# Turned blocks of three norms: through DRAM instead of sixteen moves a group

## The chip, the cores and the metric

The kernel runs on one core of one Trainium2 chip. The metric is the device time in microseconds, the median of three runs. The core has five engines that work side by side, each through its own list of instructions in order: TensorE (PE) multiplies matrices, VectorE (DVE) and ScalarE (ACT) work element by element, GpSimd (POOL) does smaller element work, and SyncE (SP) issues DMA transfers. POOL issues some transfers too. An instruction that has to wait for another engine or a transfer holds whatever stands behind it on its own engine.

## The reference

Four layers are applied to an x of 2 x 1024 tokens by 512 features, each as x + layer(layernorm(x)), in single precision:

```
x = x + attn_a(layernorm(x))     # gated linear attention in chunks of 128, 4 heads
x = x + ffn(layernorm(x))        # 512 -> 1408 -> 512, weights as codes and scales
x = x + attn_b(layernorm(x))     # softmax attention, one head of width 512
x = x + ffn(layernorm(x))        # the same weights again
ffn(x): down(silu(gate(x)) * up(x))
layernorm(x): (x - mean) / sqrt(var + 1e-5), without weights
```

The norms are called a, f, b and g after the layers that they feed.

## The kernel before, in words

Tokens are worked on in 16 tiles of 128. Four tiles make a group (index `st`, 0 to 3), two groups a pair (`pr`, 0 and 1). All products take operands with features on the partitions, so every normed tile has to be turned. Each large product splits its single-precision operand into a rounded high part and the rest (`split`, lines 75 and 76: a copy on ACT, then a subtraction on DVE that reads that copy).

The f, b and g norms are made by `ln_steps`, eight steps for each group. Four `ln_norm` steps, one for each tile, load the tile (line 102), norm it (lines 109 to 122; two tiny instructions run on POOL) and turn it on DVE in blocks of 32 x 32 (line 198). DVE turns each block where it stands, so the result `y` still has its blocks in the wrong partitions. `y` has one buffer, `[128, 4, KD, ST, 32]`: for a partition, 4 target blocks `b`, 4 feature tiles `k`, 4 tiles `i` of the group, 32 tokens `q`. Then four `ln_move` steps (`b` = 0 to 3) put the blocks in place with four transfers each, from SBUF to SBUF (line 209). Each takes 32 partitions to 32 partitions, 64 KB in runs of 32 elements. The result `xT` sits in one of 12 slots of 1 MB (`slot`), which are shared with weights and operands. SP issues the moves of a and f, of groups 0 and 1 of b, half of group 2 of b, and group 3 of g; POOL issues the others.

`combine` then forms, for a pair of groups, the operands of a scheme with seven products in place of eight. B11 and B12 are the lower half of the features of the pair's first and second group, B21 and B22 the upper halves. Its steps split B11, B21, B22 (for b also B12) and the sums T1, T2, T3, T4 into operand slots (`T_f`, `B_f` and so on in the profile); `less` (line 257) makes the sums in place in `xT` on DVE. `products` (line 338) and `score_product` (line 1023) multiply with them.

Where these steps stand in the order is written out by hand. In attention A a table (`fill`) gives each step of norm f a chunk. In the two FFNs a `plan` says how many steps follow each of the 11 blocks of hidden columns, and each of the eight output tiles. In attention B `do(norm, n)` and `do(moving, n)` place them between products. `behind(...)` puts the instructions of a step after given ones on the same engine. Within that, a planner orders every engine's instructions by a costing of its own.

The neighbours on the queues are: in attention A the row loads and the x1 stores; in the FFNs the weight loads `wcf`/`wcg` (line 327), residual loads `xrf`/`xrg` and output stores; in attention B the probabilities. Those are turned on DVE in blocks too (line 1100), stored to DRAM (`p<-py`, line 1104) and loaded back in four parts (`ptl<-p`, line 1116).

Of the kernel before, what the change touches and what calls it, by code (L numbers as in the profile page):

```python
# [9 lines left out]
F32 = mybir.dt.float32  # L10
# [6 lines left out]
P = 128  # L17
# [8 lines left out]
ST = 4  # L26
# [8 lines left out]
def hybrid_block_kernel(ctx: ExitStack, tc: tile.TileContext, a, out):  # L35
    nc = tc.nc
# [7 lines left out]
    dp = ctx.enter_context(tc.tile_pool(name="dram", bufs=1, space=bass.MemoryType.DRAM))  # L44
# [5 lines left out]
    def slot(name, dt=F32R):  # L50

        return wp.tile([P, 2048], dt, tag="slot", name=name)
# [20 lines left out]
    def split(hi, lo, src, eng=None):  # L73

        c = nc.scalar.copy(hi, src)  # L75
        return c.ins, (eng or nc.vector).tensor_tensor(lo, src, hi.bitcast(F32), ALU.subtract).ins  # L76
# [106 lines left out]
            low.dma_start(out=dst[m][:, 512:1024], in_=lo.bitcast(F32))  # L183
        return done

    lnT, lnY, lnX, laid = {}, {}, {}, []

    def ln_norm(src, nm, st, i):

# [10 lines left out]

    def ln_move(nm, st, b):

        if b == 0:
            lnT[nm, st] = slot(f"xT_{nm}{st}").rearrange("p (k c) -> p k c", k=KD)
        y = lnY[nm, st]
        xf = lnT[nm, st].bitcast(F32).rearrange("p k (i b q) -> p (k i) b q", i=ST, b=4)
        for c in range(4):
            sync = nm in "af" or (nm, st) in (("b", 0), ("b", 1), ("g", 3)) or ((nm, st) == ("b", 2) and c % 2)
            (nc.sync if sync else nc.gpsimd).dma_start(  # L209
                out=xf[32 * b : 32 * (b + 1), :, c, :],  # L210
                in_=y[32 * c : 32 * (c + 1), b].rearrange("p k i q -> p (k i) q"),
            )
# [12 lines left out]
    def ln_steps(src, nm, st):  # L225

        return [lambda i=i: ln_norm(src, nm, st, i) for i in range(ST)] + [
            lambda b=b: ln_move(nm, st, b) for b in range(4)
        ]
# [12 lines left out]
    def combine(nm, pr):  # L242


        B = {}

        def begin():
            ra, rb = (lnT[nm, 2 * pr + n].bitcast(F32) for n in range(2))
            B.update(B11=ra[:, 0:2], B12=rb[:, 0:2], B21=ra[:, 2:4], B22=rb[:, 2:4])

        def part(n, src):
            o = slot(f"{n}_{nm}{pr}").rearrange("p (s k c) -> p s k c", s=2, k=2)
            XT[nm, pr, n] = o
            split(o[:, 0], o[:, 1], B[src])

        def less(dst, x, y):
            nc.vector.tensor_tensor(B[dst], B[x], B[y], ALU.subtract)

        if nm == "b":

            return [
                lambda: (begin(), part("B11", "B11")),
                lambda: part("B21", "B21"),
                lambda: part("B12", "B12"),
                lambda: part("B22", "B22"),
                lambda: less("B11", "B12", "B11"),
                lambda: part("T1", "B11"),
                lambda: less("B12", "B22", "B12"),
                lambda: part("T3", "B12"),
                lambda: less("B22", "B22", "B11"),  # L270
                lambda: part("T2", "B22"),
                lambda: less("B21", "B21", "B22"),
                lambda: part("T4", "B21"),
            ]
        return [
            begin,
            lambda: part("B11", "B11"),
            lambda: less("B11", "B12", "B11"),
            lambda: part("T1", "B11"),
            lambda: part("B22", "B22"),  # L280
            lambda: less("B12", "B22", "B12"),
            lambda: less("B22", "B22", "B11"),
            lambda: part("T2", "B22"),
            lambda: part("T3", "B12"),
            lambda: part("B21", "B21"),
            lambda: less("B21", "B21", "B22"),
            lambda: part("T4", "B21"),
        ]
# [59 lines left out]
    with ExitStack() as actx:  # L348
# [11 lines left out]
            out=le, in_=ones, compare_op=ALU.is_ge, fill=0.0, base=0, pattern=[[1, P]], channel_multiplier=-1  # L360
# [592 lines left out]
    with ExitStack() as bctx:  # L953
# [247 lines left out]
        for b in range(NB):  # L1201
            nm, src, g = ("b", x2, 2) if b == 0 else ("g", x3, 0)
# [138 lines left out]
```

## Time and profile before

| | us |
|---|---|
| median of three runs (least, most) | 927.1 (926.89, 927.81) |
| the profiled execution | 926.9 |
| its span, from the first to the last instruction | 925.2 |
| busy: PE / DVE / ACT / POOL | 918.5 / 690.4 / 433.9 / 257.4 |
| DVE: turning a tile, line 198 (512 elements a partition) | 0.70 |
| DVE: `less`, and the low part of an operand (1024 elements) | 1.21 to 1.22 |
| ACT: the high part of an operand (1024 elements) | 1.05 |
| issue of one move, on SP / on POOL | 0.63 / 0.65 |
| issue to landing of one move of norm f on SP, median | 2.2 |

Stages by the spans of their products: attention A to 227 us, the first FFN from 227 to 442, attention B to 701, the second FFN from there. The granted TensorE clock is 1.00 throughout. In rows of groups, a name such as `xT_g<-y_g` gives what is written and what is read; SPq is SP's queue of issues. A transfer is counted as landed when its semaphore event is seen.

### The profile page before, as it was taken

To read this page: it belongs to the slowest core of one execution; us is meant where nothing else is said; L and a number is where in the kernel's file an instruction comes from. 1 tells how busy PE (TensorE), PEld (TensorE's weight loads), DVE (VectorE), ACT (ScalarE), POOL (GpSimd) and SP (SyncE) were. 2 spreads that over 40 slices of the span, in tenths; PEclk is the share of its full clock that TensorE was granted. 3 is DMA by queue.
4 is the path that set the end of the run, shared out by engine and by line. 5 is a ranking of instruction groups with operands and counts; after the bars stand their busy time and mean duration, and the time that the engine had idled before them with its cause. 6 is when DMAs were issued, how large, how long until landed. Compare 5 with 4: busy or idle time off the path is not lost.

```text
span 925.2 us, 13659 instructions
## 1 busy us (share of the span) xinstructions
PE 918.5 (99%) x4546; PEld 778.1 (84%) x4546; DVE 690.4 (75%) x1335; ACT 433.9 (47%) x928; POOL 257.4 (28%) x458
## 2 busy tenths in 40 slices
PE   9999999999999999999999999999999999999998
PEld 7899999998888888888888888888878888888887
DVE  6755657479998798778848878569968886967654
ACT  5645365556776334444234444145434444344431
POOL 4345334557563002211130401140501631001100
PEclk9999999999999999999999999999999999999999
DMA  9535655477979754724733769225969735454022
GB/s 304 210 100 124 208 160 152 158 207 262 367 236 321 214 178 153 216 47 150 281 82 83 171 168 261 69 45 137 239 140 369 259 126 137 165 205 138 22 69 80
DMA packets 216182, 162.20 MB, mean 175 GB/s; under 512 B 151024, under 2 KB 167728, under 8 KB 216112
## 3 DMA queue, kind: packets, MB, share of 16 engines
q1 hardware_dynamic: 212624, 150.05, 53.7%
q0 software_dynamic: 3488, 11.28, 4.5%
q8 instruction: 36, 0.59, 0.3%
q14 instruction: 34, 0.28, 0.1%
HBM read 104.76 MB, written 41.84 MB: 158 GB/s over the span
## 4 chain that ended last, share of the span: by engine, by line
PE 94%; DVE 2%; SPq 1%; DMA 1%; issue 1%; ACT 0%; POOL 0%; DVEq 0%; ACTq 0%
PE pXf L338 4%; PE pog L925 4%; PE pog L924 4%; PE pZf L338 4%; PE pof L925 4%; PE pXg L338 4%; PE pVg L338 4%; PE pVf L338 4%; PE pZg L338 4%; PE pof L924 4%; PE pob L91 3%; PE pob L89 3%; PE pob L90 3%; PE psZ L1023 2%; PE psX L1023 2%; PE psV L1023 2%
## 5 line engine op out<-in xcount | busy, mean ns | idle before, releaser
L924 PE MATMUL pog<-wdg,hsg 128*128 128x512 f32 (+1 forms) x165 | 60.1, 375 | 0.0
L925 PE MATMUL pog<-wdg,hsg 128*128 128x512 f32 (+1 forms) x165 | 60.0, 375 | 0.0
L925 PE MATMUL pof<-wdf,hsf 128*128 128x512 f32 x154 | 59.1, 389 | 0.0
L924 PE MATMUL pof<-wdf,hsf 128*128 128x512 f32 x154 | 58.9, 389 | 0.0
L91 PE MATMUL pob<-vh,ptl 128*128 128x512 f32 x128 | 49.9, 390 | 0.8 <-DVE ptl L76 0.8
L89 PE MATMUL pob<-vh,pth 128*128 128x512 f32 x128 | 49.9, 390 | 0.0
L90 PE MATMUL pob<-vl,pth 128*128 128x512 f32 x128 | 49.8, 389 | 0.0
L76 POOL TENSOR_TENSOR hsg<-sgg,hsg 128x128 fp32r<-128x128 f32 x40 | 18.9, 491 | 110.4 <-ACT hsg L75 102.6
L338 PE MATMUL pXg<-B_g,wcg 128*128 128x512 f32 x176 | 46.2, 389 | 0.0
L338 PE MATMUL pVf<-T_f,wcf 128*128 128x512 f32 x176 | 46.2, 389 | 0.0
L338 PE MATMUL pVg<-T_g,wcg 128*128 128x512 f32 x176 | 46.2, 389 | 0.0
L338 PE MATMUL pXf<-B_f,wcf 128*128 128x512 f32 x176 | 45.9, 390 | 0.0
L113 POOL TENSOR_SCALAR ve_g<-mv_g 128x1 f32<-128x1 f32 x16 | 7.7, 486 | 129.6 <-DVE mv_g L111 129.6
L209 POOL DMA_DIRECT2D xT_g<-y_g x48 | 31.1, 655 | 38.5 <-DVE T_b L76 29.2
L338 PEld LDWEIGHTS pXf<-B_f,wcf 128*128 128x128 f32 x176 | 32.9, 188 | 7.1 <-issue 0.3
L338 PEld LDWEIGHTS pVf<-T_f,wcf 128*128 128x128 f32 x176 | 33.0, 188 | 6.9
L338 PEld LDWEIGHTS pVg<-T_g,wcg 128*128 128x128 f32 x176 | 33.0, 188 | 6.9
L338 PEld LDWEIGHTS pXg<-B_g,wcg 128*128 128x128 f32 x176 | 33.0, 188 | 6.9
L545 ACT ACTIVATE row<-row,ncl 128x128 f32<-128x128 f32 x64 | 20.5, 391 | 35.4 <-POOL row L534 35.4
L113 POOL TENSOR_SCALAR ve_b<-mv_b 128x1 f32<-128x1 f32 x16 | 5.7, 359 | 112.4 <-DVE mv_b L111 112.2
L924 PEld LDWEIGHTS pog<-wdg,hsg 128*128 128x128 f32 x165 | 31.1, 188 | 5.7
L925 PEld LDWEIGHTS pog<-wdg,hsg 128*128 128x128 f32 x165 | 31.0, 188 | 5.6
(344 smaller groups left out, 2837.4 us busy)
## 6 DMA issues: line engine op xcount, KB each, us to landing
wcg<-wc SPq DMA_DIRECT2D x19, 896.0 KB, 5.0
wc<-wcf SPq DMA_DIRECT2D x11, 896.0 KB, 5.8
p<-py SPq DMA_DIRECT2D x15, 512.0 KB, 3.5
wcf<-wc SPq DMA_DIRECT2D x8, 896.0 KB, 6.3
ptl<-p SPq DMA_DIRECT2D x56, 128.0 KB, 3.1
xin_a<-in_x SPq DMA_DIRECT2D x16, 256.0 KB, 5.3
xra<-in_x SPq DMA_DIRECT2D x16, 256.0 KB, 3.4
row<-cl SPq DMA_DIRECT2D x16, 256.0 KB, 4.3
```

Of the source, the lines that this page charges most:

```text
L76: return c.ins, (eng or nc.vector).tensor_tensor(lo, src, hi.bitcast(F32), ALU.subtract).ins
L89: nc.tensor.matmul(ps, lhs_hi, rhs_hi, start=first, stop=False)
L90: nc.tensor.matmul(ps, lhs_hi, rhs_lo, start=False, stop=False)
L91: end = nc.tensor.matmul(ps, lhs_lo, rhs_hi, start=False, stop=last).ins
L113: nc.gpsimd.tensor_scalar(ve, mv[:, 1:2], EPS, None, ALU.add)
L209: (nc.sync if sync else nc.gpsimd).dma_start(out=xf[32 * b : 32 * (b + 1), :, c, :], in_=y[32 * c : 32 * (c + 1), b].rearrange("p k i q -> ...
L338: nc.tensor.matmul(ps, w[:, m, k * P : (k + 1) * P], o[:, s, k, :], start=first and k == 0 and s == 0, stop=k == 1 and s == 1, skip_group_ ...
L545: nc.scalar.activation(row[:, h, :], row[:, h, :], AF.Exp, bias=ncl[:, n : n + 1], scale=-1.0)
L924: nc.tensor.matmul(ps, hs[i][0][:, j], wd[j][:, ds], start=j == 0, stop=False)
L925: nc.tensor.matmul(ps, hs[i][1][:, j], wd[j][:, ds], start=False, stop=j == KH - 1)
L1023: ends[nm] = nc.tensor.matmul(ps, o[:, i, k], w[:, j, k], start=first and k == 0 and i + j == 0, stop=k == 1 and i == 1, skip_group_check= ...
```

## The change

For the norms f, b and g a group goes through a DRAM tile `[128, 4, 512]`. Each of the four `ln_move` steps now stores the 32 partitions of `y` with the same index, whole, in runs of 512 elements; the blocks are put in place by where they are stored. The fourth step also loads the 1 MB tile into a slot, in one transfer: on SP for f, on POOL for b and g. The slot is asked for at the fourth step, not at the first. In `xT` the four blocks `c` of 32 tokens now come outermost, so `combine` reads B11 and its like in a permuted view with runs of 32 elements, and `less` works in that view. The operands that it writes have the layout that they had. The moves of norm a are as before, all on SP.

```diff
-    lnT, lnY, lnX, laid = {}, {}, {}, []
+    lnT, lnY, lnX, lnD, laid = {}, {}, {}, {}, []
...
     def ln_move(nm, st, b):
 
+        y = lnY[nm, st]
+        if nm != "a":
+            if b == 0:
+                lnD[nm, st] = dp.tile([P, 4, 512], F32, tag=f"ln_{nm}{st}", name=f"ln_{nm}{st}")
+            d = lnD[nm, st]
+            nc.sync.dma_start(
+                out=d.rearrange("(b q) c f -> c q b f", b=4)[b],
+                in_=y[32 * b : 32 * (b + 1)].rearrange("p b k i q -> p b (k i q)"),
+            )
+            if b == 3:
+                lnT[nm, st] = slot(f"xT_{nm}{st}")
+                (nc.sync if nm == "f" else nc.gpsimd).dma_start(
+                    out=lnT[nm, st].bitcast(F32), in_=d.rearrange("p c f -> p (c f)")
+                )
+            return
         if b == 0:
             lnT[nm, st] = slot(f"xT_{nm}{st}").rearrange("p (k c) -> p k c", k=KD)
-        y = lnY[nm, st]
         xf = lnT[nm, st].bitcast(F32).rearrange("p k (i b q) -> p (k i) b q", i=ST, b=4)
         for c in range(4):
-            sync = nm in "af" or (nm, st) in (("b", 0), ("b", 1), ("g", 3)) or ((nm, st) == ("b", 2) and c % 2)
-            (nc.sync if sync else nc.gpsimd).dma_start(
+            nc.sync.dma_start(
...
-            ra, rb = (lnT[nm, 2 * pr + n].bitcast(F32) for n in range(2))
-            B.update(B11=ra[:, 0:2], B12=rb[:, 0:2], B21=ra[:, 2:4], B22=rb[:, 2:4])
+            ra, rb = (
+                lnT[nm, 2 * pr + n].bitcast(F32).rearrange("p (c n q) -> p n c q", c=4, q=32) for n in range(2)
+            )
+            B.update(B11=ra[:, 0:8], B12=rb[:, 0:8], B21=ra[:, 8:16], B22=rb[:, 8:16])
...
-            split(o[:, 0], o[:, 1], B[src])
+            split(*(o[:, s].rearrange("p k (i c q) -> p (k i) c q", i=ST, c=4) for s in range(2)), B[src])
```

## The prediction

> **What bounds the kernel now.** I read the busy table first, then the table of windows, PE's waits, and the chain.
>
> ```profile
> span 925.2 us, 13659 instructions
> PE 918.5 (99%) x4546; PEld 778.1 (84%) x4546; DVE 690.4 (75%) x1335; ACT 433.9 (47%) x928; POOL 257.4 (28%) x458
> ```
>
> The windows, with PE's busy time second and its count in brackets:
>
> ```profile
> 560.00:680.00 120.00, 120.00 (x531) 99.41 (x530) 89.83 (x174) 46.97 (x101) 30.05 (x48) 1.00 0.59 146
> 680.00:700.00 20.00, 19.20 (x89) 15.67 (x88) 15.95 (x23) 9.74 (x17) 0.00 (x0) 1.00 0.69 203
> ```
>
> All of PE's waits that have a releaser, with the total, the times and the longest:
>
> ```profile
> PE warm L685 <- POOL ones L356: 1.3, 1, 1.3
> PE pob L91 <- DVE ptl L76: 0.8, 1, 0.8
> ```
>
> PE is busy 918.5 of 925.2 us. The windows from 125 us, just before the first norm that the change touches, to 921 us add to 796.0 us, and PE is busy in 795.2 of them. The 0.8 us that is missing is one wait: at 684.41 us PE wants the low half of a block of probabilities (ptl), and DVE makes it late. A busy matmul engine need not run at pace, so I checked that against the chain (start, us, work):
>
> ```profile
> 679.32 1.14 DVE xT_g L257
> ...
> 755.29 1.81 PE pXg L338 x8
> ```
>
> Eight matmuls in 1.81 us is 226 ns each, and that pitch stands from 125 us to the end at a granted clock of 1.00. So no wait of any size is left for this change to remove but that one. It ends behind two steps of the changed family: the chain goes through the subtraction at L257 on xT_g at 679.32 us.
>
> The profiled execution took 926.9 us, of which 1.7 lie outside its span; the median of three runs is 927.1. I add to and take from 926.9.
>
> **The change part by part.**
>
> The moves by their line (ns least/median/most, which is the issuing engine's time), one group in the timeline, and rows of the DMA table (median us to landing):
>
> ```profile
> L209 SPq DMA_DIRECT2D xT_f<-y_f x64: 585/627/2367, 148.6 to 305.0; - x64
> L209 POOL DMA_DIRECT2D xT_g<-y_g x48: 648/648/734, 612.8 to 738.8; - x48
> ```
>
> ```profile
> 407.28 10.68 SPq L209 DMA_DIRECT2D xT_b<-y_b  x16
> ```
>
> ```profile
> x<-xra SPq DMA_DIRECT2D x16, 256.0 KB, 2.3
> p<-py SPq DMA_DIRECT2D x15, 512.0 KB, 3.5
> wcg<-wc SPq DMA_DIRECT2D x19, 896.0 KB, 5.0
> wcf<-wc POOLq DMA_DIRECT2D x3, 896.0 KB, 7.8
> ```
>
> *Removed:* 12 groups of 16 moves, 120 on SP and 72 on POOL. SP spends 10.7 us on issuing a group (the timeline's line), POOL 16 x 0.65 = 10.4, and the last move lands 2.1 to 2.9 us after its issue: 12.8 to 13.3 us from a finished y to a complete xT.
>
> *Added:* four stores of 256 KB, always on SP. The fourth is issued 3 x 0.63 = 1.9 us after the first. It lands 2.3 us later by the x1 stores, equal in bytes and direction, or 3.5 by the store of 512 KB; I take 3.0, between the two, as no row stores from 32 partitions. Then one load of 1 MB, which must wait for all four. The 896 KB loads land in 5.0 to 7.8 us; times 1024/896 that is 5.7 to 8.9, and I take 6.3 on SP and 7.5 on POOL. Sum: 1.9 + 3.0 + 6.3 = 11.2 us (f) or 12.4 us (b, g), with ends at 9.9 and 14.3. A store in a crowded stretch could take 8.7, the slowest move, which makes 20. So a group is complete at about the same time as before, and the two routes trade nothing on the path.
>
> [...] The moves here, 32 partitions each, are issued every 0.67 us and still land in 2.1, so they do overlap.
>
> *Margins.* The last data of a pair of groups, before, by the estimate, and its first reader:
> - f1: y at 186.8; before 201.1, after 199 (one other store stands between the two halves of the moves on SP); DVE reads at 201.06, having idled 1.1 us for it. PE first uses the pair at 227.
> - f3: y 289.7; before 307, after 301; read 316.8.
> - b1: y 407.2; before 420.1, after 419.6; read 423.9, PE 442.6.
> - b3: y 508.5; before 521.8, after 520.9; read after 539.
> - g1: y 654.3; before 667.6, after 666.7; read 679.24.
> - g3: y 766.2; before 784.3, after 778.6; read 789.88.
> Even 14.3 us changes no reader's start but f1's, by about a microsecond, and there DVE has 5 us between its last operand (223.8) and PE's first use of it (228.7).
>
> *Queues.* SP loses 120 issues of 0.63 and gains 48 stores and 4 loads. Where stores are new to it (b3, g0, g1, g2, half of b2) each group adds 4 x 0.63 = 2.5 us ahead of probability stores (p), their loads back (ptl), residual loads (xrb) and weight loads (wcg). SP waits idle at 508.3 to 518.4, 591.6 to 624.7, 656.8 to 661.8 (after the ptl loads) and 725.6 to 731.7 us, so they fit. An f load holds SP for some 3 us until the stores land; the twelve issues it replaces held it for 8. A load on POOL holds POOL for the same 3 us; queued behind are low halves for the down product (hsg, 0.46 each) and the next norm's rs, and the 13 moves they stood behind at 727.7 us took 8.4. After g1 POOL has nothing to do for 40.3 us.
>
> *Rooms.* The single y buffer is free about 5 us after it is full, not 13; DVE's waits for it, 0.8 and 0.9 us, go, and DVE is next held by its own queue. The slot is now taken by the load alone; in g0 POOL waited 29.2 us for one with its moves.
>
> *The permuted view.* Runs of 32 elements on DVE and ACT inputs. The transpose at L198, which reads and writes such runs, takes 0.70 us for 512 elements; the plain one at L1100 takes 1.24 for 1024. The 512 further elements cost 0.54, so 512 alone would cost 0.54 plus a fixed 0.16 and the runs add nothing; I cost them at nothing. The low end is nothing too, since the same elements are read; the high end is the 0.02 us between L198 and a plain 512-element subtraction (0.68), doubled, on 68 DVE instructions: 2.7 us of DVE spread over 650 us and hidden behind PE. ACT has no such row; I give it the same.
>
> *The order.* The planner writes every engine's order from its own costs, and these change. At the end of attention B, DVE idles from 671.18 to 673.99 us, yet the L257 step and T1's low half run at 679.24 and 681.57, 2.45 us between the maxima and the ptl halves that PE then misses. Their data had landed at 667.6. If the planner now counts the data as there sooner, these two go into the idle stretch and the 0.8 us go. If not, nothing changes. I take half, 0.4 us: the rows cannot show the planner's cost, and the ends are 0.8 and 0.
>
> [...]
>
> Sum: 926.9 - 0.4 = 926.5 us.
>
> **The rivals.**
> *PE full, little moves* (forecast): 926.1 to 927.3.
> *A late load at the end of attention B* (slower). SP is in order. If the planner sets g1's stores behind the ptl loads that SP issues from 670.18 to 675.5 rather than at 654.3, they go out by 678.5, land at 681, and the POOL load lands at 688.5. DVE reaches L257 at 679.24 and holds the maxima, the transpose and ptl behind it: 9.3 us late, 936.2. It decides from a landing after 679.24, 12.5 us later than my estimate. A load 3 us late costs about 3: 930.
> *The same at g3.* If its load stands in POOL's order behind the third wcg load, which waits for PE until 786.87, it lands at 787.4 + 7.5 = 794.9, 5.0 after its reader; the operand T is ready at 806.0 and used at 807.48, so PE loses 3.5: 930. For: POOL does wait there, 9.4 us for that load. Against: the data is free to go at 773.
> *A new order* with a wait elsewhere. Between 227 and 300 us DVE is busy nine tenths or more; one wait of 3 us there may not be hidden: 929 to 930.
> *Faster by more than 0.2%.* That needs 1.9 us, and after 125 us PE waits 0.8. It would take matmuls below 226 ns; nothing here touches them.
>
> **How the numbers follow.** This kernel's three runs spread over 0.1%; I take 0.2%, 1.85 us, as what can be told from no change. Forecast 0.61; late load at g1 0.09, at g3 0.08, a new order 0.16 (most of it at 929 to 933); faster 0.06. Same is 0.61, slower 0.33. The forecast's own range is 925.7 to 928. The 80% range reaches from 925.2, the threshold of a gain, to 932: above lie about half of the rivals' 0.33, 0.13, below about 0.05.
>
> **What would show it.** Right: PE still busy to within a microsecond from 125 us on, 48 stores landing in 2.3 to 3.5 us, loads in 5.7 to 8.9, T and B steps still 1.05 (ACT) and 1.21 us (DVE), POOL's busy time lower by about 40 us. The wait for ptl near 684 us shows whether the 0.8 went. Wrong: a wait of PE for T or B operands at the starts of FFN halves or score stages; DVE idle at L257 for the load of xT; steps above 1.3 us; p or wcg issues that start later on SP and end in a PE wait.

## The result, and the profile after

The changed kernel takes 930.77 us (median of six runs, 929.01 to 932.69) against 927.06 us (926.40 to 927.81) for the kernel before in the same session: a ratio of 1.0035, with a 95% interval of 1.0021 to 1.0049 (the two medians alone give 1.0040). The forecast was no change at 926.5 us. The time lies inside the range given (925.2 to 932.0), but the change moves it by more than the 0.2% that the prediction took for no change, and to the slower side. The profiled execution is one of the six and took 931.6 us, 0.8 more than their median.

The page of the changed kernel, its first lines, to be read against the two shown of the kernel before (span, and each engine's busy time, share and number of instructions):

```profile
span 929.9 us, 13485 instructions
PE 920.8 (99%) x4546; PEld 780.2 (84%) x4546; DVE 692.5 (74%) x1335; ACT 434.6 (47%) x928; POOL 214.2 (23%) x394
```

TensorE runs the same 4546 matmuls and is still "99% busy"; DVE and ACT are unchanged to 2.1 us, and POOL is 43 us lighter. Nothing in the busy table tells of the loss. TensorE's waits do (engine, line, releaser: total, times, longest):

```profile
PE pob L91 <- DVE ptl L76: 1.8, 1, 1.8
PE warm L702 <- POOL ones L373: 1.3, 1, 1.3
PE pS L667 <- ACT kT L641: 1.0, 2, 0.6
PE pof L941 <- ACT hsf L75: 0.7, 1, 0.7
```

The wait for ptl, which I had hoped to see go from 0.8 to 0, is 1.8 us, and there is a new one for the gated halves hsf, near 435 us. (The waits of pS and warm lie before 125 us, where the kernel before waits too.) The windows show a third thing (start:end, length, PE busy and count, PEld, DVE, ACT, POOL, then the granted clock, DMA share and GB/s):

```profile
680.00:683.00 3.00, 1.37 (x5) 1.14 (x6) 2.96 (x7) 0.60 (x2) 0.00 (x0) 0.91 0.23 87
683.00:686.00 3.00, 3.00 (x9) 2.33 (x8) 1.23 (x5) 3.00 (x10) 0.00 (x0) 0.52 0.01 3
686.00:690.00 4.00, 4.00 (x24) 3.36 (x23) 2.86 (x6) 1.18 (x3) 0.00 (x0) 1.00 0.45 135
```

From 0.8 us after the end of the wait TensorE is granted half its clock. In the trace's clock records the stretch is 682.45 to 685.86 us, 3413 ns; eight matmuls in it start 427 ns apart instead of 227, 1.6 us lost while PE counts as fully busy.

To find all such losses I took, over the whole trace, each matmul's distance to the next one's start and subtracted the median for its shape. Summed, this lost time is 9.5 us after and 5.6 before. The 4 us between them are: the end of attention B 2.6 (3.66 against 1.08, wait and half clock together; 1.6 of it is the half clock, which four of the six runs seem not to have had, as the last section shows), the wait at 434.8 us 1.0, and 0.45 ahead of 150 us, where the two programs had nothing of the change to do yet. The time from the last matmul to the end of the span adds 0.75 (4.45 against 3.70): the last store of the output lands that much later, for which I have no reason. Of the kernels below, those with the new route for both f and b show it too (4.31 to 4.46), all but one (3.86, stores on POOL); the others end 3.69 to 3.95 us after the last matmul.

Why ptl is late is in DVE's timeline of the changed kernel (start, us, instruction; the idle time before it and its releaser in brackets):

```profile
671.15 0.68 DVE L1060 TENSOR_TENSOR upb<-psV,upb 128x512 f32<-128x512 f32 x1
674.96 1.23 DVE L274 TENSOR_TENSOR xT_g<-xT_g,xT_g 128x1024 f32<-128x1024 f32 x1 [3.12 <-DMA xT_g<-ln_g]
677.30 1.23 DVE L76 TENSOR_TENSOR T_g<-xT_g,T_g 128x1024 fp32r<-128x1024 f32 x1 [1.12 <-ACT T_g L75]
678.45 0.74 DVE L1161 SCALAR_TENSOR_TENSOR xrb<-pob,ri,xrb 128x512 f32<-128x512 f32 x1
...
680.90 1.28 DVE L76 TENSOR_TENSOR ptl<-ptl,pth 128x512 fp32r<-128x512 f32 x2
```

The same steps in the kernel before:

```profile
673.99 0.75 DVE L1144 SCALAR_TENSOR_TENSOR xrb<-pob,ri,xrb 128x512 f32<-128x512 f32 x1 [2.80 <-PE pob L91]
...
679.24 1.22 DVE L257 TENSOR_TENSOR xT_g<-xT_g,xT_g 128x1024 f32<-128x1024 f32 x1
...
681.57 1.23 DVE L76 TENSOR_TENSOR T_g<-xT_g,T_g 128x1024 fp32r<-128x1024 f32 x1 [0.73 <-ACT T_g L75]
...
684.87 1.28 DVE L76 TENSOR_TENSOR ptl<-ptl,pth 128x512 fp32r<-128x512 f32 x2
```

The planner did what I had given half a chance: it moved the subtraction and T1 of the pair g1 (formerly at 679.24 and 681.57) into the stretch where DVE has nothing to do, ahead of a residual (xrb11), the last maxima and ptl. But g1's load lands at 674.93, not at 666.7. DVE, in order, stands 3.1 us with all of these queued behind it. SP's timeline shows where the data was (L1162 stores a residual, L210 the four new stores):

```profile
654.96 3.27 SPq L1133 DMA_DIRECT2D ptl<-p  x4
658.33 0.72 SPq L1162 DMA_DIRECT2D x<-xrb  x1
659.14 2.92 SPq L210 DMA_DIRECT2D ln_g<-y_g  x4
```

and POOL's where the load was issued:

```profile
666.97 0.62 POOL L216 DMA_DIRECT2D xT_g<-ln_g  x1 [15.22 <-DMA xrb<-x]
```

The y of g1 is complete at 656.86, 2.5 us later than in the kernel before (654.34). The stores start 2.3 us after it, behind the residual's. The fourth goes out at 660.82 and lands 5.4 us later, at 666.18. POOL's load goes out at 666.97, 6.15 us after the fourth store, and lands 8.0 later. (The page names the load of xrb as POOL's last releaser; what POOL needs is the four stores, and its waits for them end from 666.21 on.) From y to xT 18.1 us, not 12.4.

### The profile page after: what moved, and what is told of

Same layout as the page of the kernel before. It is cut to its first block, busy times and chain, and to the rows that moved or that the text cites. A ratio compares the mean times of both kernels' runs of the same rounds, so it can differ in the third digit from the quotient of the medians.

```text
span 929.9 us, 13485 instructions
## 1 busy us (share of the span) xinstructions
PE 920.8 (99%) x4546; PEld 780.2 (84%) x4546; DVE 692.5 (74%) x1335; ACT 434.6 (47%) x928; POOL 214.2 (23%) x394
## 4 chain that ended last, share of the span: by engine, by line
PE 91%; DVE 3%; DMA 3%; SPq 2%; ACT 1%; issue 1%; POOL 0%; DVEq 0%; ACTq 0%; POOLq 0%
PE pog L942 4%; PE pog L941 4%; PE pof L941 4%; PE pXf L355 4%; PE pof L942 4%; PE pZg L355 4%; PE pZf L355 4%; PE pVg L355 4%; PE pXg L355 4%; PE pVf L355 4%; PE pob L91 3%; PE pob L89 3%; PE pob L90 3%; PE pYf L355 2%; PE pYg L355 2%; PE psZ L1040 2%
## 5 line engine op out<-in xcount | busy, mean ns | idle before, releaser
L76 POOL TENSOR_TENSOR hsg<-sgg,hsg 128x128 fp32r<-128x128 f32 x40 | 18.1, 472 | 128.2 <-ACT hsg L75 82.5
L941 PEld LDWEIGHTS pof<-wdf,hsf 128*128 128x128 f32 x154 | 28.9, 188 | 7.1 <-ACT hsf L75 1.1
L942 PEld LDWEIGHTS pof<-wdf,hsf 128*128 128x128 f32 x154 | 28.9, 188 | 6.0
```

The lines of the kernel that those rows point to most:

```text
L941: nc.tensor.matmul(ps, hs[i][0][:, j], wd[j][:, ds], start=j == 0, stop=False)
L942: nc.tensor.matmul(ps, hs[i][1][:, j], wd[j][:, ds], start=False, stop=j == KH - 1)
```

## The experiments

The two theories at the outset: (1) the loss is mostly the late load of g1, met by two steps that now stand at a place where DVE needs it 7 us earlier than before, with the half clock as its sequel, and the wait at 435 us the rest; (2) it is the new route itself, its traffic in twelve groups or its groups of norm b. All ratios are to the kernel before, beside it on the same chip; 0.1% is 0.93 us.

**The route for norm g alone, and for f and b alone.**

```diff
-        if nm != "a":
+        if nm in "g":        # in the second kernel: "fb"
```

(The other norms keep the sixteen moves, their queues and their unpermuted views.)

> The new route for norm g alone; f and b keep the sixteen moves and their queues. Theory 1 (the loss is mostly the late load of g1 at the end of attention B: DVE stands at the first subtraction for it, PE then waits about 2 us for the low half of the probabilities, and 3.4 us at half clock follow): the ptl wait of 1.5 us or more and the stretch at half clock come back, the shift at 435 us does not; 929 to 930. Rival 1 (the traffic of stores and loads in all twelve groups costs a little everywhere): a third of the loss, about 928.2, without the half clock. Rival 2 (the cost is that of the norm b groups, where PE loses 0.9 us near 435 us): 927.

> The new route for norms f and b alone; g keeps its moves. Theory 1: the end of attention B is as in the kernel before (ptl wait 0.8 us or none, clock 1.0 there); what remains is the 0.9 us near 435 us: 927 to 928. Rival 1 (traffic everywhere): two thirds of the loss, about 929.5. Rival 2 (norm b): the whole loss, about 930.5.

Measured: g alone 1.0026 (1.0015 to 1.0038), 929.97 us; f and b 1.0017 (1.0008 to 1.0025), 929.58 us. With g alone the ptl wait is 1.9 us and the half clock follows again, for 3413 ns; the wait at 435 us is gone. With f and b the end of attention B is as before, and the wait at 435 us is there. So the two losses belong to different norms. For f and b, 1.6 us is more than theory 1 gave: the trace has the 1.0 at 435 us, one more wait of 0.57 at 213 us, in attention A, and 0.6 more behind the last matmul.

**The two steps taken away from that place, the route left as it is.**

```diff
-                if b:
-                    with behind(summed):
-                        do(moving, 2)
...
         with behind(splits):
-            do(moving, 6)
+            do(moving, 8)
```

> The changed kernel, with the first subtraction and T1 of the pair g1 no longer drawn ahead of the last low halves of the probabilities: all eight of the pair's steps stand behind the last of them. The route, its stores and loads stay. Theory 1: the load of g1 may land as late as it does and nothing of attention B stands behind it: ptl wait at most 0.8 us, no stretch at half clock, 2.6 us less than the changed kernel: about 928. Rival (the route's traffic, or the order elsewhere): 930.8 as the changed kernel. A third case: the two steps are then missed later, and PE waits for the operand T of the first g half at about 690 to 700 us: 929 or more with that wait.

Measured: 1.0009 (1.0000 to 1.0018), 928.28 us. No wait for ptl, no half clock; g1's load goes out at 667.35, 0.4 us later than in the changed kernel. 2.6 thousandths of the 3.5 are gone, 2.4 us, the wait of 0.8 us that the kernel before has among them. This bears theory 1 out, but alone it does not tell whether the place or the late data does the harm.

**The same place in the kernel before, with data that is early.**

First with the two steps behind the last residual (xrb11) and ahead of the maxima:

```diff
+            made[:] = split(o[:, 0], o[:, 1], B[src])
...
+            with behind(ahead):            # ahead = what T1's split issued
+                array(scores_tail, b, n)
```

> The kernel before, moves and queues untouched, with the subtraction and T1 of g1 put where the changed kernel has them: right behind the last residual, ahead of the last maxima. There the moves have landed at 667.6 us. Theory 1 (the early place does harm only because the data comes late on the new route): the step starts without a wait, the ptl wait goes: 926.0 to 926.8. Rival (the early place itself delays the maxima and the ptl halves): PE's ptl wait grows to 2 us and the half clock appears: 929 to 930.

Then ahead of that residual, where the changed kernel has them:

```diff
+            with behind(made if t == NT - 5 else ()):
+                end = nc.vector.scalar_tensor_tensor(xr, po, ri, xr, ALU.mult, ALU.add).ins
...
+            with behind(ahead):            # ahead = that residual
+                array(scores_tail, b, n)
```

> The kernel before, moves untouched, with the subtraction and T1 of g1 not behind the last residual as in the run before this one but ahead of it, right behind upb13: exactly where the changed kernel has them on DVE; TensorE's order is unchanged. The moves land by about 668, DVE is free from 671.2. Theory 1, mended (the place is harmless if the data is there when DVE falls idle, and costs what it runs past the idle stretch): the 3.5 us of the two steps run from 671.2 to 674.7, the residual is 0.7 us later than now, no wait for ptl or one under 0.8 us: 926.5 to 927.8, as the kernel before or 1 us better. Rival (the place harms whatever the data does): ptl wait of 1.8 us or more, 930 to 931.

Both expectations failed: 1.0036 (1.0023 to 1.0050) and 1.0033 (1.0021 to 1.0045), as slow as the changed kernel, with old moves that POOL had issued by 667.9 us. In the first the residual itself waits for TensorE until 675.42, the idle stretch is over, and the two steps with their wait for ACT simply stand in front of the maxima for 3.5 us; TensorE waits 2.8 us. In the second the subtraction runs in the idle stretch, and then:

```profile
673.02 1.22 DVE L257 TENSOR_TENSOR xT_g<-xT_g,xT_g 128x1024 f32<-128x1024 f32 x1
678.72 1.23 DVE L76 TENSOR_TENSOR T_g<-xT_g,T_g 128x1024 fp32r<-128x1024 f32 x1 [4.48 <-ACT T_g L75]
```

T1's low half needs ACT's copy of T1, and in the order that the planner wrote for ACT here that copy stands behind the copy of pth, which waits for a load:

```profile
676.59 1.14 ACT L75 CAST pth<-ptl 128x512 fp32r<-128x512 f32 x2 [5.17 <-DMA ptl<-p]
677.64 1.04 ACT L75 CAST T_g<-xT_g 128x1024 fp32r<-128x1024 f32 x1
```

So neither is the clean copy of the changed kernel's place that I meant it to be, and they decide nothing about the data. What they do show is that this spot forgives nothing: with the two steps ending late, for two other reasons, they are 3.3 and 3.1 us slower.

**The data early, by another queue.** The four stores of g1 alone go out from POOL, which is idle there:

```diff
-            nc.sync.dma_start(
+            (nc.gpsimd if (nm, st) == ("g", 1) else nc.sync).dma_start(
```

> The changed kernel with one edit: the four stores of group g1 go out from POOL, which is idle there, and not from SP, where they stood 2.3 us behind a residual's store and were spread over 1.7 us more. Every engine's order of computing stays as in the changed kernel. Theory 1: stores issued from 657 to 659, landed by 664, load landed by 672; DVE's wait of 3.1 us for it falls to under 0.7, ptl wait under 0.8, no stretch at half clock: about 928.3, as the run with the steps behind the ptl halves. Rival (the place or the traffic, not the lateness): 930.5 to 931.

Measured: 1.0028 (1.0017 to 1.0039), 930.36 us: the edit did not do what it was for. The stores start 0.3 us after y instead of 2.3, but then take longer to land, and so does the load:

```profile
657.89 2.30 POOL L210 DMA_DIRECT2D ln_g<-y_g  x4 [5.42 <-DVE y_g L198]
666.36 0.56 POOL L216 DMA_DIRECT2D xT_g<-ln_g  x1 [6.16 <-DMA ln_g<-y_g]
```

DVE waits until 676.12 for it, 18.5 us after y; TensorE waits 1.3 us for pth and 0.7 for ptl. The earlier issue alone did not bring the data sooner. In the changed kernel the mean busy share of the DMA engines, as the profile counts it, is 0.99 from 650 to 680 us (0.90 before), with the loads of ptl, a residual and the norm's inputs beside these stores, and full DMA engines could be the reason. But here the share is 0.70 from 663 to 665 us and 0.46 from 665 to 667, while POOL's waits for the last stores end at 665.7 and later; for the load it is 0.93 to 1.06. So full engines do not explain the slow stores, for the load they may, and no run took traffic away: the cause stays open.

**The wait taken away, nothing else.** The first subtraction of the pair g1 reads g0's own quarter twice and so can run without g1's load (the difference is then zero, and T1 lacks that data). Stores, load and the order on all engines are those of the changed kernel:

```diff
-            lambda: less("B11", "B12", "B11"),
+            lambda: less("B11", "B11" if pr == 0 and nm == "g" else "B12", "B11"),
```

> The changed kernel with one operand changed: the first subtraction of the pair g1 takes group g0's own quarter twice, so it no longer waits for g1's load; the load, the stores and every engine's order stay. The result of that quarter is left wrong. Theory 1 (the late data at that place is the cause): DVE's wait of 3.1 us there goes, the two steps lie in the idle stretch, the ptl wait is at most 0.8 us, no half clock: 928.2, as the run with the two steps moved behind the ptl halves. Rival (the place itself, with ACT's copy ahead of pth, costs it whatever the data does): ptl or pth wait of 1.5 us or more, 930 to 931.

Measured: 1.0014 (1.0005 to 1.0023), 928.65 us. The steps now lie in the idle stretch, and ptl starts 2.5 us earlier:

```profile
671.45 1.21 DVE L274 TENSOR_TENSOR xT_g<-xT_g 128x1024 f32<-128x1024 f32 x1
673.78 1.23 DVE L76 TENSOR_TENSOR T_g<-xT_g,T_g 128x1024 fp32r<-128x1024 f32 x1 [1.11 <-ACT T_g L75]
675.07 0.75 DVE L1161 SCALAR_TENSOR_TENSOR xrb<-pob,ri,xrb 128x512 f32<-128x512 f32 x1
...
678.40 1.28 DVE L76 TENSOR_TENSOR ptl<-ptl,pth 128x512 fp32r<-128x512 f32 x2
```

TensorE waits for ptl no more. This is the run that tells place and data apart: the place that the planner chose was a good one, for data that is there; the late load makes it a bad one. 2.1 thousandths of 3.5 go with that one operand. What is left in this run and in the one with the steps late is in their traces: 1.0 us at 435 us, 0.57 at 213, and 0.6 to 0.8 behind the last matmul, less what the kernel before loses for ptl.

**The wait for ptl made longer.** Two maxima that nothing reads, put ahead of the low half in the kernel before:

```diff
+            held_up = list(after)
+            if b * NK + i == NT - 3:
+                for n in range(2):
+                    with behind(held_up):
+                        held_up = [
+                            nc.vector.tensor_reduce(
+                                mp.tile([P, 1], F32, tag="nm", name=f"spin{n}"), pes[NT - 2][0][:, 0:512], AX.X, ALU.max
+                            ).ins
+                        ]
+            with behind((*after, *held_up)):
```

> The kernel before, with two maxima of 512 elements that nothing reads, 0.6 us apart on DVE, ahead of the low half that TensorE waits for at 684 us: the wait grows from 0.8 to about 2.0 us and nothing else changes. [...] Rival (the half clock has nothing to do with the wait): +1.2 us, 929.

Measured: 1.0042 (1.0026 to 1.0059), 931.71 us, 3.9 us more; five of the six runs lie between 931.4 and 933.9. The profiled run has the wait of 2.0 us and no half clock. The rest of its time is elsewhere: TensorE waits 1.3 us for a weight load (wcg) at 699 us and 0.8 for hsg near 805 us, which SP and DVE brought later. So 1.2 us at this spot cost more than 1.2, by waits further on. Of the six runs one has a mean clock (0.998) that speaks of a stretch at half clock; that a wait of 2.0 us brings one is not shown here.

**f and b alone.** The same one-line edit as the first pair, for "b" and for "f".

> The new route for norm b alone. If the 0.9 us wait near 435 us (TensorE waits for ACT's copy of the last gated halves of norm f's second half of the FFN) comes from b's groups, whose copies then stand elsewhere in ACT's order: the wait is there, and the time is about 928.7. If it comes from f's groups or only with both: not there, 927.8 as before.

> The new route for norm f alone. By the runs with f and b together (1.8 us slower) and with b alone (2.1 us slower) f costs nothing: 927 to 928. If the wait at 435 us comes from f's order as well: 928.5 to 929.

Measured: b 1.0018 (1.0009 to 1.0026), f 1.0026 (1.0016 to 1.0035). With b the wait at 435 us is there (0.98 us lost), and 0.8 more at the end of attention B, where pth comes a little late. With f it is not, but another is, at 382 to 391 us, which the changed kernel does not have:

```profile
PE pXf L363 <- DMA wcf<-wc: 1.4, 2, 1.0
```

My expectation for f, nothing, was wrong: the cost of norms does not add up. f and b together (1.0017) are no slower than f alone. SP's timelines show why this wait is the mixture's own: with f alone the load of wcf goes out at 376.59 us, between two rows of eight old moves of b, and lands at 383.63, when TensorE has begun to wait (in the kernel before it goes out at 374.58 and TensorE does not wait). In the changed kernel the same load goes out at 363.82, ahead of b's stores. Each mixture has another order, and an order can have a place of its own where TensorE waits a microsecond.

**The two steps late in other mixtures.** Four kernels, each with the two steps behind the ptl halves by the second edit above: the kernel before; and, by the first edit, the new route for f and g (`if nm in "fg"`), for g, and for b and g.

> The kernel before, with the subtraction and T1 of g1 moved behind the last ptl halves, as in the changed kernel's run with all eight steps there. Theory 1: these two steps are what holds ptl up in the kernel before also; its wait of 0.8 us goes: 926.4 to 927, faster than before by 0.4 to 1 us. Rival (the wait has another cause, or the steps are then missed at the start of the FFN): as before or slower.

> The new route for norms f and g, the old moves for b, and g1's two steps behind the ptl halves. If b's groups cost the wait at 435 us and g's cost what the two steps did, nothing is left: 926.5 to 927.5, as before or a little better. If the route's traffic costs something of its own: 928.5 or more.

> The new route for norm g alone, with g1's two steps behind the ptl halves. If the route of g's four groups (its stores, loads and the fuller DMA engines) costs nothing of itself and only the two steps did: 927 to 928, no wait of TensorE over 0.5 us after 125 us, as the kernel before. If the traffic itself costs: 929 or more.

> The new route for norms b and g, the old moves for f, g1's two steps behind the ptl halves. If b's groups bring the wait of 0.9 us near 435 us by the order that the planner writes, it is there again, alone, and the time is about 1 us above the run with g alone: 928 to 929. If that wait needs f's groups too: as the run with g alone.

Measured: before 0.9995 (0.9985 to 1.0004), f and g 1.0008 (0.9999 to 1.0017), g 0.9996 (0.9986 to 1.0006), b and g 0.9995 (0.9987 to 1.0004). With g alone the route costs nothing that shows once the two steps stand elsewhere. With b and g the wait at 435 us is back (0.98 us lost) without f, but the microsecond that I expected it to add does not show in the ratio. With f and g the waits for wcf appear (1.5 us lost), and the median, 928.80 us, is above what I expected if nothing was left. None is shown to beat the kernel before: each interval takes in no change. I had expected a gain for the kernel before with the steps late, and the ptl wait of 0.8 us is indeed gone in all four (f and g lose 0.5 us near by).

All of it in one table: the time that TensorE lost by the matmuls' pitch in three stretches of each profiled run, its sum after 150 us, and the ratio measured. The kernel before has a sum of 0.7.

| kernel | 370-400 | 430-440 | 670-692 | sum after 150 us | ratio |
|---|---|---|---|---|---|
| before | 0.2 | 0.0 | 1.1 | 0.7 | 1 |
| changed | 0.0 | 1.0 | 3.7 | 4.2 | 1.0035 |
| g | 0.0 | 0.0 | 3.8 | 3.3 | 1.0026 |
| f, b | 0.0 | 1.0 | 1.1 | 2.1 | 1.0017 |
| b | 0.0 | 1.0 | 1.9 | 2.3 | 1.0018 |
| f | 1.9 | 0.0 | 1.1 | 2.7 | 1.0026 |
| changed, steps late | 0.0 | 1.0 | 0.0 | 1.0 | 1.0009 |
| changed, no wait | 0.0 | 1.0 | 0.0 | 1.1 | 1.0014 |
| changed, stores on POOL | 0.0 | 1.0 | 2.5 | 3.2 | 1.0028 |
| before, steps late | 0.1 | 0.0 | 0.0 | -0.4 | 0.9995 |
| g, steps late | 0.5 | 0.0 | 0.0 | -0.2 | 0.9996 |
| b, g, steps late | 0.0 | 1.0 | 0.0 | 0.3 | 0.9995 |
| f, g, steps late | 1.5 | 0.0 | 0.5 | 2.7 | 1.0008 |
| before, steps ahead of the maxima | 0.0 | 0.0 | 3.0 | 2.5 | 1.0036 |
| before, steps ahead of the residual | 0.0 | 0.0 | 4.9 | 4.2 | 1.0033 |
| before, ptl held up | 0.4 | 0.0 | 2.3 | 5.0 | 1.0042 |

The sums, less 0.7, agree with the measured differences to about 1.5 us; each is one execution, and the time behind the last matmul is not in them. Every kernel with the new route for b loses 0.97 to 0.99 us between 430 and 440 us, and no other one does. That this is b's doing is shown; which step of the order makes it was not tried.

## Why the prediction was wrong

**What bounds the kernel.** Right, with a gap: TensorE full from 125 us, nothing to win but 0.8. I drew from it that little can be lost either. The runs show the other side: near 684 us there was no slack at all, and two steps that ended late there cost 3 us.

**"The order", taken as 0.4 us of gain between 0.8 and 0.** This is the step that failed. The mechanism was the right one, and half my chance on it was well spent: the planner did pull the step and T1 into the idle stretch. The bounds were wrong. I reasoned that the data had landed at 667.6 in the kernel before and would land at 666.7, so the move could only help or do nothing; its loss end was left out. One comparison was missing: the step's place moves from 679.2 to 671.8, so a landing after about 672, not after 679.24, decides; "even 14.3 us changes no reader's start but f1's" had every reader stay where it was. My estimate was 5 us ahead of that, and its own upper end of 20 us for a crowded stretch (a landing at 674) was already past it. Measured: in place of a gain of 0.8 at most, the end of attention B lost 2.6 us more than before in the profiled run, 1.0 by the longer wait and 1.6 by the half clock behind it. The run without the wait is 2.0 us faster than the changed kernel, the run with the steps late 2.4.

**The group's 12.4 us (b, g), 11.2 (f).** Too short at every store. The DMA table of the changed kernel (kilobytes each, median us to landing):

```profile
ln_f<-y_f SPq DMA_DIRECT2D x16, 256.0 KB, 4.5
xT_f<-ln_f SPq DMA_DIRECT2D x4, 1024.0 KB, 6.0
ln_b<-y_b SPq DMA_DIRECT2D x16, 256.0 KB, 4.2
xT_b<-ln_b POOLq DMA_DIRECT2D x4, 1024.0 KB, 5.4
ln_g<-y_g SPq DMA_DIRECT2D x16, 256.0 KB, 4.9
xT_g<-ln_g POOLq DMA_DIRECT2D x4, 1024.0 KB, 5.8
```

Stores land in 4.2 to 4.9 us by their medians (2.6 to 6.1 over all 48) where I took 3.0 with a high end of 3.5, from stores that read all 128 partitions and go out one or two at a time. Whether the 32 partitions or the four in a row make them slower was not tried. The loads are on the mark or quicker by their medians (5.4 to 6.0 for 6.3 and 7.5), though g1's took 8.0. At f1 the whole route, from the first store at 187.34 to the end of DVE's wait at 202.08, took 14.7 us, 3.5 more than my 11.2. The four stores overlap and are down 7.2 us after the first was issued, and the load takes 7.3. At g1, with 18.1 us, the estimate was short by 5.7. In the changed kernel's trace f1 delayed only DVE, as predicted (1.6 us of idle against 1.1). But in four other kernels with the new route for f, where DVE idles 2.2 to 2.8 us there, TensorE waits 0.4 us for kT at 213 us; in the three where DVE idles 1.5 to 1.9, the changed kernel among them, it does not.

**The queues: "SP waits idle … 656.8 to 661.8 …, so they fit".** They fit, but not when wanted: SP is in order, and the stores stood behind a residual's store that held SP until 659.1. The kernel before has that store too, in the stretch that the prediction counts as idle:

```profile
656.78 0.85 SPq L1145 DMA_DIRECT2D x<-xrb  x1
```

That is 2.3 of the 5.7 us by which g1's route was longer than the estimate; from the first store to the load it took 2.9 more, the load 0.5. Another 2.5 us of the late landing (674.93 for 666.7) are not the route's: y itself was that much later in the new order, where the prediction kept y's time.

**The late load at the end of attention B, given 0.09.** This is what came, by another door: not because the stores stood behind the ptl loads, but because the reader moved forward. Its price, "a load 3 us late costs about 3: 930", is near the 930.8 measured, in part by luck: DVE waited 3.1 us, but the 930.8 hold the wait at 435 us and the later end as well, and the half clock, which the price did not know, in some runs.

**A new order with a wait elsewhere, 0.16.** Came too, at 435 us, for 1 us.

**Slips that move nothing.** Two rows of TensorE's waits, of 0.5 and 0.4 us, are missing where "all" are said to be shown; they lie before 125 us. The wait for ptl begins at 684.81, behind the matmul that starts at 684.41. Half of 0.33 is 0.17, not the 0.13 put above the range.

**Right:** the steps cost what they did to 0.01 us (ACT 1.05, DVE 1.22: the permuted view is free; only B_f's low halves are longer, 1.29 for 1.21), POOL is 43 us lighter, the y room no longer holds DVE (0.2 us in all), g3's load was in time, and the route of g by itself is worth nothing on the path: with g alone and the steps late the ratio is 0.9996. For f that is not shown: f alone is at 1.0026.

## What to carry to other kernels

A margin belongs to a pair, a landing and the place of its reader. When something else writes the order (a planner, a scheduler, one's own list), a change of the landing's cost also moves the reader, so the margin must be taken against the earliest place to which the reader may be drawn, not against where it stands today. A step that is pulled into an idle stretch of an in-order engine carries its wait with it: if the data isn't there, all that the engine has queued behind it is late (DVE stood 3.1 us here), and the possible loss belongs in the sum beside the possible gain. And where the bounding engine is full, parts of a change need not add (f alone 1.0026, f and b 1.0017): here each mixture got its own order with its own lost microsecond, so a part tried alone said little on the whole.

## What was not expected of the hardware

The half clock. In three traces (the changed kernel, g alone, and the kernel before with the steps ahead of the residual) TensorE's wait at the end of attention B, idle for 1.9, 2.1 and 3.2 us (the distance of two starts less the usual one), was followed by a stretch of exactly 3413 ns at a granted clock of 0.5, 1.6 us lost each time:

```profile
681.63 0.50 PE L91 MATMUL pob<-vh,ptl 128*128 128x512 f32 x1 [1.77 <-DVE ptl L76]
...
683.69 0.63 PE L91 MATMUL pob<-vh,ptl 128*128 128x512 f32 x1
684.12 0.63 PE L89 MATMUL pob<-vh,pth 128*128 128x512 f32 x1
684.54 0.63 PE L90 MATMUL pob<-vl,pth 128*128 128x512 f32 x1
```

In two others, idle for 2.9 us (steps ahead of the maxima) and 2.2 us (ptl held up), it was not. The clock's records begin on a grid of 3413.3 ns that is the same from a run's first record to its last, and that lies differently in the two runs given here (changed kernel: 6.61, 682.45, 685.86; the distances are 198 and 1 steps; kernel before: 4.99 and 926.59, 270 steps).

| kernel | idle from | to | idle, us | half clock |
|---|---|---|---|---|
| changed | 679.70 | 681.63 | 1.9 | yes |
| g | 677.95 | 680.00 | 2.1 | yes |
| before, steps ahead of the residual | 679.30 | 682.45 | 3.2 | yes |
| before, steps ahead of the maxima | 679.76 | 682.69 | 2.9 | no |
| before, ptl held up | 685.19 | 687.34 | 2.2 | no |

So the length of the idle time does not tell the two kinds apart: 1.9 us was followed by a half clock, 2.9 us was not, and neither were the 1.8 us of two waits in the run with the stores on POOL. What decides it was not shown.

That the half clock comes with these waits, in some runs and not in others, the mean clocks of all runs show. A stretch of 3413 ns at half clock takes 0.002 off a run's mean (half of 3.413 us, of some 930). Of the 47 runs of the six kernels with 1.8 us or more of waits there (the five of the table and the stores on POOL) 19 have a mean of 0.998 or 0.997; of 204 runs of the kernel before and of the other nine kernels none has. In the changed kernel it is two of six, those of 931.6 and 932.69 us (0.997), against 929.01 to 930.89 us for the rest (0.999 and 1.0). Runs with such a mean are 1.7 to 2.4 us slower on average in four of the six kernels, and no slower in the other two.
